# Row maxima of the first kv head moved into the projection, with two instead of three sets of query stacks

## The chip, the cores and the metric

The kernel runs on one core of a Trainium2 chip. The metric is the device time of one execution in microseconds (us); lower is better. TensorE (PE) multiplies matrices and writes to PSUM, VectorE (DVE), ScalarE (ACT) and GpSimd (POOL) work on tiles in SBUF, and SyncE (SP) issues most DMA transfers between DRAM and SBUF. Each engine works through its own instructions in their order and waits on semaphores for the others.

## What is computed

The reference is one transformer block on x of 2 x 1024 x 1024, fp32. Cut to what matters:

```python
xn = layernorm(x)                       # over the last axis
q = xn @ wq; k = xn @ wk; v = xn @ wv   # 32 query heads, 8 kv heads, 32 wide
q, k = rope(q), rope(k)                 # positions 0..1023
scores = q k^T / sqrt(32) + causal mask # four query heads share one kv head
s = (softmax(scores) @ v) @ wo
g = silu(ffn(xn))                       # gated, 4-bit weights with scales per group of 128
out = x + s * g
```

## The kernel before

The two sequences go through the same stages one after the other: `norm` (L301), `project` (L325), `attend` (L393) and `project_out` (L700). The feed-forward part follows for both together. The order of instructions in `norm`, `project` and `project_out` is set by a scheduler that puts ready work on each engine. In `attend` the order is the order of the code (`tc.manual_schedule()`).

**Projection.** The columns are done in ten blocks of 128: two for k, then v, then eight for q. `turned` does a k or q block in two halves of 512 tokens: eight fp32 products into one of three PSUM banks (`ps_qk`, L350), the rotation (two DVE instructions, L352 and L354, two on POOL, L355 and L356), a rounding to fp32r on ACT (`rot_hi`, L358), its remainder on DVE (`rot_lo`, L360), and two stores to DRAM (L361, L362), from SP. A score is computed from both parts. For the feed-forward part, xn is stored in two parts as well (`x_hi`, `x_lo`). In the first sequence, `look` prepares the scales of the 4-bit weights between the blocks (its tiles in `prep_ps`).

**Attention.** One of the eight kv heads is a round of its own, called a head here; its four query heads are j = 0 to 3. The scores need stacks: `kst_g`, the head's keys in 128 rows (both parts, each twice), and `qst_0` to `qst_3`, the four query heads' queries in 128 rows. They are loaded from DRAM by SP, four transfers of 128 KB for a tile (L414 and L422). The pool `at_q` holds three sets of the four query tiles (`bufs=3`, L402).

The softmax needs a shift for each row ahead of the exponential. `maxima` (L461 to L474) computes the scores with queries in rows: 48 units for a head, each one product (`s`) into one of two PSUM banks, on the diagonal a product that adds the mask (L470), and a row maximum on DVE (L474). `shifts` (L483 to L488) turns the maxima into three bf16 parts (`mt`), and `shift_rows` transposes them (`m_ps`, L502) and copies them to `mrow` (L506).

The head itself has 12 steps (qb, kt): two blocks of 512 queries, and the key tiles of 128 that each one sees (4 and 8). A step does the scores with keys in rows (`st`, L531, mask L540; one PSUM bank for each j), the product that adds the shifts (`weights`, L549), the exponential on ACT (L559), and, one step later, the product with v (`values`, L570). Sums for the denominator (`total`, L587) follow some steps later.

Into these steps the next head's maxima are woven. `turn` (L643) is called behind each score product and at the end of a step; it takes maxima units as long as a planned rate allows. So while head g computes, its DVE reductions and 48 units are for head g+1. The query stack of head g+1 is asked for at the start of head g. SP runs ahead of the other engines: such a load goes out as soon as its buffers are free. With three sets, the set of stack g+1 is that of stack g-2.

The maxima of head 0 have no head to be woven into. They run on their own, behind the projection:

```python
kst = [key_stack(0)]
stack = {0: stacks(0)}
for g in range(1, NKV):
    kst.append(key_stack(g))
mx = maxima_tile()
for _ in maxima(0, stack[0], mx):
    pass
box = [shift_rows(shifts(mx))]
```

Of the kernel before, what the change touches and what calls it, by code (L numbers as in the profile page):

```python
# [23 lines left out]
P = 128  # L24
# [12 lines left out]
def block_kernel(  # L37
# [141 lines left out]
    def scales_turned(pool, psp):  # L179
# [10 lines left out]
        ps = psp.tile([P, NF, 2, G_GU], F32, name="ps_sc")  # L190
# [14 lines left out]
        ps = psp.tile([P, NC, G_D], F32, name="ps_sd")  # L205
# [7 lines left out]
    def look(pool, psp):  # L213
# [19 lines left out]
        ps = psp.tile([1, 1], F32, name="ps_bad")  # L233
# [91 lines left out]
    def project(b, xnT, qs, ks, v, side):  # L325


        with tc.tile_pool(name="qkv_w", bufs=3) as wp, tc.tile_pool(name="qkv", bufs=3) as pool, tc.tile_pool(
# [16 lines left out]
            def turned(w, dst):  # L345
                for n in range(NB):
                    tok = slice(n * TB, (n + 1) * TB)
                    ps = psp.tile([P, TB], F32, name="ps_qk")
                    for s in range(NS):
                        nc.tensor.matmul(ps, w[:, s, :], xnT[:, s, tok], start=(s == 0), stop=(s == NS - 1))  # L350
                    t1 = pool.tile([P, TB], F32, name="rot1")
# [23 lines left out]
            for c in range(2):  # L375
                turned(following(), ks[c])
            for t in range(NT):
                ps = vps.tile([P, N_KV * HD], F32, name="ps_v")
                for s in range(NS):
                    nc.tensor.matmul(  # L380
                        ps, xnT[:, s, t * P : (t + 1) * P], w[:, s, :], start=(s == 0), stop=(s == NS - 1)
                    )
                nc.scalar.copy(v[:, t, :], ps)
            for c in range(NC):
                turned(following(), qs[c])
# [5 lines left out]
                nc.sync.dma_start(xs_dram[b][1, :, c, :], lo.bitcast(F32))  # L391

    def attend(qs, ks, v, oT):  # L393
# [5 lines left out]
        with ExitStack() as st:  # L399
            st.enter_context(tc.manual_schedule())  # L400
            kp = st.enter_context(tc.tile_pool(name="at_k", bufs=1))
            qp = st.enter_context(tc.tile_pool(name="at_q", bufs=3))  # L402
            pp = st.enter_context(tc.tile_pool(name="at_p", bufs=7))
            mp = st.enter_context(tc.tile_pool(name="at_m", bufs=1))
            sm = st.enter_context(tc.tile_pool(name="at_s", bufs=2))
            ps_s = st.enter_context(tc.tile_pool(name="ps_s", bufs=2, space=PSUM))
            ps_t = st.enter_context(tc.tile_pool(name="ps_t", bufs=1, space=PSUM))
            ps_o = st.enter_context(tc.tile_pool(name="ps_o", bufs=1, space=PSUM))

            def key_stack(g):  # L410
                k = kp.tile([P, T], F32R, name=f"kst_{g}")
                rows = slice(HD * (g % 4), HD * (g % 4 + 1))
                for i in range(4):
                    nc.sync.dma_start(k[HD * i : HD * (i + 1), :].bitcast(F32), ks[g // 4][i // 2, rows, :])  # L414
                return k

            def stacks(g):
                out = []
                for j in range(NREP):
                    q = qp.tile([P, T], F32R, name=f"qst_{j}")  # L420
                    for i in range(4):
                        nc.sync.dma_start(  # L422
                            q[HD * i : HD * (i + 1), :].bitcast(F32), qs[g][i % 2, HD * j : HD * (j + 1), :]
                        )
                    out.append(q)
                return out

            class Clock:  # L430
                pe = act = dve = 0.0
                bank = [0.0, 0.0]
                st = [0.0] * NREP

                def product(self, w, n=1.0, switch=False):
                    self.pe += 15.0 + 0.416 * n * w + (90.0 if switch else 0.0)

                def take(self):
                    self.pe = max(self.pe, self.bank[0])

                def read(self, ns):
                    self.dve = max(self.dve, self.pe + 180.0) + ns
                    self.bank = [self.bank[1], self.dve + 60.0]

                def exp(self, j, w):
                    self.act = max(self.act, self.pe + 180.0) + 170.0 + 0.84 * w
                    self.st[j] = self.act + 60.0

            clock = Clock()

            def maxima(g, q, mx):

                for qt in range(NT):
                    nk = (qt + 1) * P
                    for h, k0 in enumerate(range(0, nk, TB)):
                        k1 = min(nk, k0 + TB)
                        for j in range(NREP):
                            s = ps_s.tile([P, TB], F32, name="s")
                            diag = k1 == nk
                            clock.take()  # L460
                            nc.tensor.matmul(  # L461
                                s[:, : k1 - k0],
                                q[j][:, qt * P : (qt + 1) * P],
                                kst[g][:, k0:k1],
                                start=True,
                                stop=not diag,
                            )
                            clock.product(k1 - k0)
                            if diag:
                                nc.tensor.matmul(  # L470
                                    s[:, k1 - k0 - P : k1 - k0], ident_r, mask_q, start=False, stop=True
                                )
                                clock.product(P)
                            nc.vector.tensor_reduce(mx[:, qt, j, h : h + 1], s[:, : k1 - k0], AX.X, ALU.max)  # L474
                            clock.read(158.0 + 1.04 * (k1 - k0))
                            yield k1 - k0 + P

            def shifts(mx):


                mt = next(mts)
                nm = [sm.tile([P, NT, NREP, 2], F32, name=f"nm_{t}") for t in range(2)]
                nc.vector.tensor_reduce(nm[0][:, :, :, 0], mx, AX.X, ALU.max, negate=True)  # L483
                for t in range(3):
                    nc.vector.tensor_reduce(mt[:, :, :, t], nm[t % 2][:, :, :, :1], AX.X, ALU.max)
                    if t < 2:
                        nc.vector.tensor_reduce(nm[t][:, :, :, 1], mt[:, :, :, t : t + 1], AX.X, ALU.max, negate=True)
                        nc.vector.tensor_reduce(nm[1 - t][:, :, :, 0], nm[t], AX.X, ALU.add)  # L488
                clock.dve += 1700.0
                return mt  # L490

            mts = [mp.tile([P, NT, NREP, HD], BF16, name=f"mt_{i}") for i in range(2)]
            for mt in mts:
                nc.gpsimd.memset(mt, 0.0)
            mts = itertools.cycle(mts)

            def shift_rows(mt):
                mrow = mp.tile([P, T], BF16, name="mrow", bufs=2)
                for h in range(NB):
# [136 lines left out]
            for _ in maxima(0, stack[0], mx):  # L636
                pass
# [667 lines left out]
```

## Time and profile before

| what | us |
|---|---|
| runs of the kernel | 2524.58, 2527.64, 2533.06 |
| median of the runs | 2527.64 |
| the profiled execution, its own time | 2529.01 |
| its span in the trace | 2527.1 |

The mean granted clock of TensorE in the profiled execution is 0.959 of full speed. Times in the trace count from the start of the span. The page gives busy times of the engines, 40 slices of the span (in tenths, with the granted clock as PEclk), the chain of work that ended last, and groups of instructions. The trace behind it answers for a window, a tile or an engine's waits. The stages of the first sequence, by the trace: the last product of the projection ends at 201.84, the first score product of head 0 starts at 257.31, the first one of head 1 at 308.76, and project_out's products run from 642 to 752. In the second sequence, the projection's last product ends at 960.25 and the first score product starts at 1018.71.

### The profile page before, as it was taken

The page shows a single profiled execution, that of the slowest core. Times are in us where ns is not written, and L with a number is a line of the kernel's source. Part 1 is how long each engine was busy: PE and PEld are TensorE (multiplying, and loading weights), DVE is VectorE, ACT ScalarE, POOL GpSimd, SP SyncE. Part 2 cuts the span into 40 slices and gives each one's busy share as a digit, 9 for nine tenths or more (in the row PEclk, how much of TensorE's full clock was granted, in tenths as well). Part 3 has the DMA queues.
Part 4 walks back from the last instruction along what each step waited for, and adds up shares of the span by engine and source line. Part 5 has one row for each costly group of instructions (what it writes and reads, how often), then busy time and mean ns, then how long its engine had stood idle before and what let it go on. Part 6 is the DMA issues. An engine that isn't in the chain of part 4 may idle for free.

```text
span 2527.1 us, 32374 instructions
## 1 busy us (share of the span) xinstructions
PE 2402.1 (95%) x12130; PEld 1673.6 (66%) x12130; DVE 1407.3 (56%) x2176; ACT 1144.3 (45%) x1824; POOL 708.6 (28%) x449
## 2 busy tenths in 40 slices
PE   7997999999996996999999999999999999999997
PEld 4643565665784643565565787888887888888865
DVE  6144566663224234566663026676787777767865
ACT  2010344445343100344445135555578755556875
POOL 1231355546331231354546110000024400000352
PEclk8996899999997996899999999999999999999999
DMA  7357111200997327111110863222174655423465
GB/s 225 113 200 188 34 37 34 52 17 1 275 301 233 127 102 175 34 51 34 40 29 1 283 216 92 75 75 72 54 283 156 216 152 142 117 67 98 131 201 164
DMA packets 262350, 309.61 MB, mean 123 GB/s; under 512 B 18283, under 2 KB 202987, under 8 KB 262040
## 3 DMA queue, kind: packets, MB, share of 16 engines
q1 hardware_dynamic: 250964, 269.00, 36.0%
q0 software_dynamic: 9472, 33.83, 4.2%
q10 hardware_dynamic: 1748, 4.62, 0.6%
q8 instruction: 98, 1.61, 0.3%
q14 instruction: 68, 0.56, 0.1%
HBM read 214.58 MB, written 97.03 MB: 123 GB/s over the span
## 4 chain that ended last, share of the span: by engine, by line
PE 83%; DMA 6%; POOL 3%; issue 3%; DVE 2%; ACT 2%; SPq 1%; ACTq 0%; POOLq 0%; DVEq 0%
PE acc L984 25%; PE ps_qk L350 11%; PE acc L867 11%; PE s L461 9%; PE st L531 6%; PE o L570 5%; PE ps_wo L714 3%; DMA ng<-nf 3%; PE l L587 2%; PE ps_v L380 2%; PE st L549 2%; PE s L470 2%; PE st L540 1%; DVE mx L474 1%; DMA xt<-in_L_attn_x 1%
## 5 line engine op out<-in xcount | busy, mean ns | idle before, releaser
L984 PE MATMUL acc<-x,w 128*128 128x512 f32 x2752 | 640.0, 393 | 1.5 <-ACT gate L955 0.9
L984 PEld LDWEIGHTS acc<-x,w 128*128 128x128 f32 x2752 | 512.4, 188 | 120.7 <-DVE h L957 7.2
L474 DVE TENSOR_REDUCE mx<-s 128x1 f32<-128x512 f32 (+3 forms) x768 | 408.7, 556 | 257.9 <-PE s L470 196.8
L559 ACT ACTIVATE p<-st 128x512 f32<-128x512 f32 (+3 forms) x768 | 314.8, 497 | 510.6 <-PE st L549 507.2
L756 DVE TENSOR_SCALAR acc<-acc,r_gu 128x1024 f32<-128x1024 f32 x301 | 389.1, 1293 | 160.2 <-PE acc L984 158.1
L672 POOL TENSOR_TENSOR p<-p 128x1536 f32<-128x1536 f32 (+3 forms) x126 | 371.5, 2948 | 374.2 <-PE s L470 128.6
L754 ACT ACTIVATE acc<-acc,r_gu 128x1024 f32<-128x1024 f32 x301 | 327.5, 1088 | 230.3 <-PE acc L984 225.5
L461 PE MATMUL s<-kst,qst 128*128 128x512 f32 (+3 forms) x768 | 326.0, 444 | 43.5 <-DMA qst<-qs 37.7
L968 POOL TENSOR_TENSOR h_lo<-h,h_hi 128x512 fp32r<-128x512 f32 x78 | 100.3, 1287 | 820.9 <-PE acc L867 588.9
L461 PEld LDWEIGHTS s<-kst,qst 128*128 128x128 f32 x768 | 153.0, 202 | 216.4 <-issue 82.6
L350 PE MATMUL ps_qk<-xnT,w_qk 128*128 128x512 f32 x640 | 278.7, 596 | 0.7 <-ACT xnT L323 0.7
L756 DVE TENSOR_SCALAR acc<-acc,r_d 128x512 f32<-128x512 f32 x320 | 241.7, 759 | 67.1 <-PE acc L867 64.7
L531 PE MATMUL st<-qst,kst 128*128 128x512 f32 (+3 forms) x768 | 270.1, 385 | 2.8 <-ACT p L559 2.7
L754 ACT ACTIVATE acc<-acc,r_d 128x512 f32<-128x512 f32 x320 | 210.8, 662 | 65.6 <-PE acc L867 58.7
L867 PE MATMUL acc<-h_lo,w 128*128 128x512 f32 (+1 forms) x576 | 228.9, 397 | 2.9 <-POOL h_lo L968 2.6
L867 PE MATMUL acc<-h_hi,w 128*128 128x512 f32 (+1 forms) x576 | 229.5, 398 | 0.7 <-ACT h_hi L967 0.7
L714 PE MATMUL ps_wo<-oT,w_o 128*128 128x256 f32 x1024 | 226.6, 385 | 3.1 <-DVE oT L622 1.7
L350 PEld LDWEIGHTS ps_qk<-xnT,w_qk 128*128 128x128 f32 x640 | 122.2, 191 | 151.6 <-issue 149.7
L714 PEld LDWEIGHTS ps_wo<-oT,w_o 128*128 128x128 f32 x1024 | 197.7, 193 | 32.0 <-DVE oT L622 2.5
L531 PEld LDWEIGHTS st<-qst,kst 128*128 128x128 f32 x768 | 145.7, 192 | 41.7 <-ACT p L559 31.5
L570 PE MATMUL o<-p,v 128*32 128x512 f32 (+3 forms) x1536 | 164.6, 499 | 0.0
L358 ACT CAST rot_hi<-rot 128x512 fp32r<-128x512 f32 x40 | 24.7, 618 | 236.7 <-POOL rot L356 228.9
(154 smaller groups left out, 2198.1 us busy)
## 6 DMA issues: line engine op xcount, KB each, us to landing
w<-ng SPq DMA_DIRECT2D x86, 512.0 KB, 5.0
qst<-qs SPq DMA_DIRECT2D x256, 128.0 KB, 3.7
w<-nd SPq DMA_DIRECT2D x63, 512.0 KB, 3.6
ng<-nf POOLq DMA_DIRECT2D x42, 512.0 KB, 5.5
x<-xs SPq DMA_DIRECT2D x32, 512.0 KB, 6.8
xt<-in_L_attn_x SPq DMA_DIRECT2D x16, 512.0 KB, 5.1
w_qk<-in_L_attn_wq SPq DMA_DIRECT2D x16, 512.0 KB, 6.6
xs<-x_hi SPq DMA_DIRECT2D x16, 512.0 KB, 6.5
```

The lines of the kernel that those rows point to most:

```text
L350: nc.tensor.matmul(ps, w[:, s, :], xnT[:, s, tok], start=(s == 0), stop=(s == NS - 1))
L461: nc.tensor.matmul(s[:, : k1 - k0], q[j][:, qt * P : (qt + 1) * P], kst[g][:, k0:k1], start=True, stop=not diag,)
L474: nc.vector.tensor_reduce(mx[:, qt, j, h : h + 1], s[:, : k1 - k0], AX.X, ALU.max)
L531: nc.tensor.matmul(s[:, q0:], kst[g][:, kt * P : (kt + 1) * P], stack[g][j][:, qlo + q0 : qlo + TB], start=True, stop=False,)
L559: nc.scalar.activation(p[:, j, q0:], st[j][:, q0:], AF.Exp, scale=1.0 / math.sqrt(HD))
L570: nc.tensor.matmul(o[HD * j : HD * (j + 1), q0:], v[:, kt, HD * g : HD * (g + 1)], p[:, j, q0:], start=(kt == 0), stop=last,)
L672: what(*args)
L714: nc.tensor.matmul(ps[:, c, :], ws[c][:, g, :], oT[:, g, t0 : t0 + BLK], start=(g == 0), stop=(g == NS - 1))
L754: nc.scalar.mul(a, a, r)
L756: nc.vector.tensor_scalar(a, a, r, None, ALU.mult)
L867: nc.tensor.matmul(acc[c], w[:k, c * P : (c + 1) * P], ht[:k, :], start=(f == 0 and t == 0), stop=(t == 1), skip_group_check=(f > 0),)
L984: nc.tensor.matmul(a[:, n, :], w[i][:, g * P : (g + 1) * P], xs[t][:, g, n * TB : (n + 1) * TB], start=(g == 0 and t == 0), stop=(t == 1), ...
```

## The change

- The code of the maxima, the shifts and the loads of stacks moves out of `attend` into a class `Maxima`. Its tiles (`mt`, `kst_0`, a set `qst_0` to `qst_3`, `mx`, `nm`, `mrow`) lie in a pool `at_first`, opened before `norm`, and so do its two PSUM banks (`ps_s`). The fills of `mt` on POOL come before the projection.
- `project` loads `kst_0` behind the k blocks and the query stack of head 0 behind the first q block. From the third q block on, `turned` takes one maxima unit of head 0 after every second of its eight products. That is 48 units in six blocks. Then the shifts and `shift_rows` follow.
- The three PSUM tiles of `look` share one bank.
- `attend` starts with head 0's tiles given. It loads stack 1 first, then the keys of heads 1 to 7. `at_q` has two sets instead of three; the set of head 0 isn't used again. The stack of head g+1 is asked for at the start of head g for g of 1 and more.
- `turn` takes no units in steps 0, 1 and 2 of head 0 (`first_turn = 3`, counted over all steps).
- The pools of `attend`, of `project_out` (`wo`, `wo_ps`) and of `unpack` get `reuse_waits="tile"`: a tile waits for the users of its own bytes in what lay there earlier, and not for those of the whole pool.

In the lines of the changed kernel, the product of a unit is L477, its mask L486, its row maximum L488, the transposes of shifts L512, the copies to `mrow` L516, the loads of stacks L439 (keys) and L444 (queries), the score products L568 and L577, the shift product L586, the exponential L596, the products with v L607.

```diff
-            def turned(w, dst):
+            def turned(w, dst, work=iter(())):
                 for n in range(NB):
...
                     for s in range(NS):
                         nc.tensor.matmul(ps, w[:, s, :], xnT[:, s, tok], start=(s == 0), stop=(s == NS - 1))
+                        if s % 2:
+                            next(work, None)
...
             for c in range(2):
                 turned(following(), ks[c])
+            head.keys()
...
+            work = head.rows()
             for c in range(NC):
-                turned(following(), qs[c])
+                turned(following(), qs[c], work if c > 1 else iter(()))
+                if c == 0:
+                    head.queries()
...
+            for _ in work:
+                pass
...
+        def keys(self):
+            self.key_stack(0, self.k)
+
+        def queries(self):
+            self.query_stack(0, self.q)
+
+        def rows(self):
+
+            mx = self.tile()
+            yield from self.turns(self.k, self.q, mx)
+            mt = self.shifts(mx)
+            yield
+            self.rows_0 = self.shift_rows(mt)
...
-            kp = st.enter_context(tc.tile_pool(name="at_k", bufs=1))
-            qp = st.enter_context(tc.tile_pool(name="at_q", bufs=3))
-            pp = st.enter_context(tc.tile_pool(name="at_p", bufs=7))
...
+            kp = st.enter_context(tc.tile_pool(name="at_k", bufs=1, reuse_waits="tile"))
+            qp = st.enter_context(tc.tile_pool(name="at_q", bufs=2, reuse_waits="tile"))
+            pp = st.enter_context(tc.tile_pool(name="at_p", bufs=7, reuse_waits="tile"))
...
-            kst = [key_stack(0)]
-            stack = {0: stacks(0)}
-            for g in range(1, NKV):
-                kst.append(key_stack(g))
-            mx = maxima_tile()
-            for _ in maxima(0, stack[0], mx):
-                pass
-            box = [shift_rows(shifts(mx))]
+            stack = {0: head.q, 1: stacks(1)}
+            kst = [head.k] + [key_stack(g) for g in range(1, NKV)]
+            box = [head.rows_0]
...
-                while done < upto and most and clock.bank[0] <= clock.pe + 250.0:
+                while i >= first_turn and done < upto and most and clock.bank[0] <= clock.pe + 250.0:
...
+            first_turn = 3
             for i, (g, qb, kt) in enumerate(steps):
                 if qb == 0 and kt == 0:
                     if g + 1 < NKV:
-                        stack[g + 1] = stacks(g + 1)
-                        mx = maxima_tile()
-                        work = maxima(g + 1, stack[g + 1], mx)
+                        if g:
+                            stack[g + 1] = stacks(g + 1)
+                        mx = head.tile()
+                        work = head.turns(kst[g + 1], stack[g + 1], mx)
...
-        with tc.tile_pool(name="wo", bufs=NC) as wp, tc.tile_pool(name="wo_ps", bufs=2, space=PSUM) as psp:
+        with tc.tile_pool(name="wo", bufs=NC, reuse_waits="tile") as wp, tc.tile_pool(name="wo_ps", bufs=2, space=PSUM, reuse_waits="tile") as psp:
```

## The prediction, made before the changed kernel ran

> **What bounds the kernel now.** I read the page's busy times and slices first: TensorE is busy for 95% of the span, so the question is where the other 5% lies, and where TensorE is slow rather than idle.
>
> ```profile
> PE 2402.1 (95%) x12130; PEld 1673.6 (66%) x12130; DVE 1407.3 (56%) x2176; ACT 1144.3 (45%) x1824; POOL 708.6 (28%) x449
> ...
> PE   7997999999996996999999999999999999999997
> ...
> PEclk8996899999997996899999999999999999999999
> ```
>
> A slice is 63 us. The fourth (190 to 253 us) and the sixteenth (948 to 1011 us) lose both in busy time and in granted clock: these are the two entries into attention, one for each sequence. The list of TensorE's waits names what ends last there:
>
> ```profile
> PE s L461 <- DMA qst<-qs: 37.7, 8, 15.9
> ```
>
> 37.7 us in 8 waits, the longest 15.9: the maxima products wait for the query stacks to come back from DRAM. The chain of what ended last, in order of time, tells the first entry step by step (start, length, what):
>
> ```profile
> 194.95 6.88 PE ps_qk L350 x16
> 201.88 1.38 POOL mt L494 x2
> ...
> 207.68 2.04 DMA qs<-rot_lo
> ...
> 216.71 4.29 DMA qst<-qs
> ...
> 252.90 1.35 DVE mx L474 x2
> 256.51 1.03 PE m_ps L502 x8
> ```
>
> From the projection's last product (201.8) to the first transposes of the shifts (256.5) nothing runs that a head would count as progress, except the maxima. The windows by stage give clock and busy time (length; busy time of PE, weight load, DVE, ACT, POOL; granted clock; DMA share; GB/s):
>
> ```profile
> 202.00:257.00 55.00, 33.31 (x85) 20.94 (x86) 30.06 (x60) 1.90 (x2) 4.28 (x6) 0.55 0.85 201
> 257.00:268.00 11.00, 10.33 (x47) 7.09 (x45) 2.02 (x6) 3.70 (x8) 0.10 (x1) 0.50 0.00 0
> 268.00:600.00 332.00, 330.63 (x2468) 198.81 (x2467) 208.40 (x428) 146.54 (x354) 171.18 (x75) 1.00 0.13 33
> 643.00:648.00 5.00, 5.00 (x15) 4.02 (x14) 0.00 (x0) 0.00 (x0) 0.00 (x0) 0.56 1.20 290
> ```
>
> The entry runs at clock 0.55, and the next 11 us still at 0.50. After that the heads are bound by TensorE alone: busy 330.6 of 332 us at clock 1.00. Any wait put on TensorE there is a loss in full.
>
> **Part 1, the entry: what it gives.** I measure from the last ps_qk product (call it T) to the first score product of step 3 of head 0, since steps 0 to 2 are where the order changes. Before, that is 201.84 to 271.98, 70.1 us, for the first sequence and 960.25 to 1033.31, 73.1 us, for the second.
>
> After, the maxima, the key stack and the query stack are there already. What is left behind T: the rotation of the last block. Before, it ended at T+5.8 (rot_lo, 206.96 + 0.69), with the 1.38 us of the two fills of mt ahead of it on POOL, which now run before the projection; the shifts' rows (two copies, 0.76 us) stand behind it on DVE: T+6 to 7. The exponential's buffer lies on bytes that the last rot_lo store reads, which lands 2.04 us after its issue: T+8.3; ACT's table load (1.28 us at 206.95) comes next: first exponential at T+9.6. Before, 11.3 us lay between it (260.68) and step 3, with 11 maxima products of head 1 among them at half clock; without them, some 8, so T+18. There the first maxima product of head 1 needs stack 1 and kst_1: 20 transfers of 128 KB, issued from T+6.3; before, a stack's 16 issues took 8.3 us and each landed 3.3 us later, 20 thus 10.4 + 3.3 = 13.7: T+20. Then the 11 deferred products (0.25 us each, 2.75) and, since the clock comes back at T+26 at the earliest (6 us of dense work after T+20), 3 us lost to half clock: 25.75. Gain 44.4 us and 47.3 us.
>
> **What it costs in the projection.** The 48 maxima products and their masks now stand between ps_qk products, which were dense (81.8 of 82.0 us busy, clock 1.00), so they add in full. Start to start in the heads they take 0.23 us at 128 columns, 0.24 at 256, 0.29 at 384, 0.35 at 512 with a mask, 0.245 without: 13.0 us for 48. DVE must then read them: 48 reductions, 26.6 us by 0.29, 0.42, 0.55 and 0.69 each, in blocks where it was busy for 36 of 82 us. It has room, but there are two banks for s, and a rot_lo that waits on DVE for POOL and ACT holds the reductions behind it. In the first sequence some products stand in clumps around the preparation of scales. I take 4 us for that in the first sequence and 2 in the second (bounds: nothing, and 13.6, all that DVE's 26.6 exceed 13.0). Sums 17 and 15. Net gain 27.4 + 32.3 = 59.7; bounds 45 to 75.
>
> The fills of mt, the pools opened early and the shared prep_ps bank I cost at nothing: POOL is busy for 31 and ACT for 12 of 82 us of the projection. The looser waits of w_o and unpack I cost at nothing too: project_out's own products are dense from 642 to 752 us while its transfers fill 0.9 to 1.2 of the DMA engines, and the first w_o loads still wait for the last readers of attention.
>
> **Part 2, two buffers for the stacks: what it takes.** at_q goes from 3 to 2 sets. Set 0 of the first head now lies elsewhere, so stack 1 and 2 take the two, and stack 3 must wait until stack 1 is read for the last time: by the last step of head 1. Its maxima products stand in TensorE's queue right behind the first score product of head 2. So, too, stacks 4 to 7: five boundaries in each sequence, ten in all. Before, the same load was released one head (48 us) earlier than needed. The trace of before shows such a load (which nobody waited for then) beside the products that will wait for it:
>
> ```profile
> 306.56 0.33 PE L531 MATMUL st<-qst,kst 128*128 128x128 f32 x1
> 306.92 4.94 SPq L422 DMA_DIRECT2D qst<-qs  x11
> 309.25 0.33 PE L461 MATMUL s<-kst,qst 128*128 128x128 f32 x1
> 311.00 0.27 PE L461 MATMUL s<-kst,qst 128*128 128x128 f32 x1
> 311.31 0.39 PE L549 MATMUL st<-mrow,ones_b 32*128 32x512 bf16 x4
> ```
>
> The last reads of the old stack (306.56 to 307.28) release the issues; all 16 go out in 8.34 us (306.92 to 315.26), and each lands 3.1 to 3.6 us after its issue. The fourth tile is there at 318.2 or so; the product that reads it stood at 311.0. Queued behind it on TensorE are the weights of step 0 and everything else of the head: 7.2 us per boundary. The products of the three earlier tiles run singly meanwhile, one or two per 2 us.
>
> Then the clock. Where TensorE was busy for 4.3 of 9 us (634 to 643) the mean granted clock was 0.67, and the dense products after it ran at 0.56 for five more (window above); full clock came back after 4.4 to 6.8 us of dense work in six such places. Half of 5.6 us is 2.8. Per boundary 10.0, ten times 100 us. Bounds: the wait from 4.1 (16 issues at 0.303 us, as key stacks' have them, are out after 4.85 us and the last lands 3.3 later, at 315.1) to 8.8 (if transfers land after 4.5 us, as key stacks' did), the clock from nothing to 3.4: 4.1 to 12.2, or 41 to 122 in all. I take 10.0, as the row for the wait is the very load.
>
> The Trainium skill, page "TensorE: Matmul & The Clock Gate", section "Part 1: The HAM clock gate (the "warmup" mystery)", says that about 3.4 us of sustained work bring the full clock back. The trace's 4.4 to 6.8 are longer; by the page's figure each boundary would lose an estimated 1.7 us to the clock and not 2.8, and the time would be 11 us less. The page "Trainium Kernel Development and Optimization", section "Best Practices", asks for double buffers, by which two sets would do; the row above speaks against it, because a set comes free only in the instant in which the next one's first reader starts, and by the page the ten boundaries would cost nothing.
>
> **Sum.** 2529.0 (the profiled execution) - 59.7 + 100 = 2569.3. The median of the runs shown is 1.4 below the profiled execution; so 2568.
>
> **Rivals.**
> - The stalls come, but the single products keep the clock up: 7.2 x 10 = 72, net +12, 2540. For it: tiles land some 2 us apart, so TensorE is never idle for long at a stretch. Against: the half-busy stretch from 634 to 643 us.
> - DVE becomes the bound in the projection: all 13.6 us show in each sequence, 27 in place of 6: 2589. With bigger boundaries beside it, up to 2603. For it: rot_lo in front of reductions; against: DVE is busy for under half of that stage.
> - The other side: the stall is short, because the loads are released and land in time. The place is SP's queue at the five boundaries; it decides under 6.0 us per boundary (59.7 / 10). At the low bound of 4.1 the time is 2509, with no stall 2468. For it: key stacks' issues are that quick. Against: the release is the last read, and the row's load of 8.34 us ran with the DMA engines nearly idle (share 0.13), so little is left to speed it up.
> - The change doesn't do what it says: the maxima wait in the projection for their own stack, and TensorE stalls there instead (no gain, 100 lost): 2628. Against: two blocks, 27 us, lie between the store of head 0's queries and the first maxima product, and a stack needs 2 + 8.3 + 3.3.
>
> **Chances.** Forecast 0.60, clock up 0.13, DVE bound 0.13, short or no stall 0.10, no gain 0.04. About 0.3% (7.6 us) is what a measurement can tell from no change. Faster by more: 0.08 (most of the short-stall case); within: 0.06 (the rest of it and the lower end of the clock case); slower: 0.86. The range 2530 to 2603 leaves out the short stall, the no-gain case and a few ends of the others.
>
> **What would show it.** Right: TensorE's waits in the profile after have a line s <- DMA qst at L477 with some 10 to 40 waits and 60 to 85 us; PEclk falls below 9 in slices inside the heads; the first exponential of head 0 starts 9 to 11 us after the last ps_qk; the projection from block 2 on is 15 to 19 us longer; POOL and DVE don't become releasers there. Wrong: no such line inside the heads (then it is faster by about 60), or a wait of ps_qk or s for DVE of over 10 us in the projection. What would make it wrong most likely is the size of the stall at a boundary, since every microsecond there counts ten times.

## The result, and the profile after

| what | us |
|---|---|
| runs of the changed kernel | 2566.63, 2567.66, 2568.96, 2571.19 |
| their median | 2568.31 |
| median of the kernel before, run beside it | 2530.35 |
| ratio | 1.0154, 95% interval 1.0131 to 1.0177 |
| profiled execution after: its time, its span, mean granted clock | 2566.63, 2564.8, 0.954 |

The changed kernel is 38 us slower than before. The forecast was 2568, with a range of 2530 to 2603.

The page of the changed kernel, busy tenths and granted clock in 40 slices (a slice is 64 us now):

```profile
PE 2409.3 (94%) x12130; PEld 1690.3 (66%) x12130; DVE 1401.4 (55%) x2176; ACT 1144.5 (45%) x1824; POOL 708.5 (28%) x449
...
PE   7998998899996998999989999999999999999997
...
PEclk8998999889997998989999999999999999999999
```

The two dips at the entries have become shallower: slice 4 has 8 tenths instead of 7, slice 16 has 8 instead of 6, and their clocks are 8 instead of 6. In their place the heads show busy tenths of 8 in slices 7, 8 and 21 and clocks of 8 in slices 8, 9 and 18, where before there were only nines. TensorE's waits name what stands there:

```profile
PE s L477 <- DMA qst<-qs: 51.5, 40, 2.0
...
PE s L477 <- DMA kst<-ks: 9.4, 2, 6.1
```

Before, the first line read 37.7 us in 8 waits, the longest 15.9. Now it is 40 short ones. That is ten boundaries with four query tiles each, and no wait for a stack of head 0 is left. The timeline at one of them, the boundary of heads 2 and 3 of the first sequence (start, length, engine, line; in brackets the idle time before the instruction and what ended it):

```profile
385.65 7.26 SPq L444 DMA_DIRECT2D qst<-qs  x16
...
387.07 0.62 PE L512 MATMUL m_ps<-ident_b,mt 128*128 128x128 bf16 x8
387.50 0.48 PE L568 MATMUL st<-qst,kst 128*128 128x512 f32 x1
...
389.87 0.30 PE L477 MATMUL s<-kst,qst 128*128 128x128 f32 x1 [1.83 <-DMA qst<-qs]
...
392.07 0.30 PE L477 MATMUL s<-kst,qst 128*128 128x128 f32 x1 [1.45 <-DMA qst<-qs]
...
394.33 0.44 PE L477 MATMUL s<-kst,qst 128*128 128x128 f32 x1 [1.46 <-DMA qst<-qs]
...
396.44 0.44 PE L477 MATMUL s<-kst,qst 128*128 128x128 f32 x1 [0.82 <-DMA qst<-qs]
...
397.04 0.61 PE L586 MATMUL st<-mrow,ones_b 32*128 32x512 bf16 x4
```

The load of stack 4 goes out at 385.65, when head 2 reads stack 2 for the last time. Each of the four tiles is awaited singly. The fourth product stands at 396.44, that is 9.4 us behind the transposes of the boundary (m_ps, 387.07). Before, it stood 2.7 us behind them: the prediction shows it at 311.00, and the transposes were here:

```profile
308.33 0.62 PE L502 MATMUL m_ps<-ident_b,mt 128*128 128x128 bf16 x8
```

So 6.7 us are lost up to the fourth product. Over the ten boundaries its place is 9.5 us behind the transposes in the mean, and 2.7 before: 6.8 us. The windows of the same stretch (granted clock third from the end, then DMA share and GB/s) show what comes on top:

```profile
386.00:390.00 4.00, 2.17 (x27) 1.39 (x27) 0.76 (x2) 0.79 (x4) 3.53 (x3) 1.00 0.86 220
390.00:394.00 4.00, 1.42 (x8) 0.88 (x8) 0.58 (x2) 0.00 (x0) 0.00 (x0) 0.83 0.99 234
394.00:398.00 4.00, 2.85 (x18) 1.74 (x18) 0.58 (x2) 0.32 (x1) 0.00 (x0) 0.50 0.32 71
398.00:402.00 4.00, 4.00 (x23) 3.84 (x17) 1.70 (x4) 2.22 (x5) 0.00 (x0) 0.50 0.01 4
402.00:406.00 4.00, 4.00 (x29) 2.77 (x28) 2.14 (x4) 1.64 (x4) 0.73 (x1) 0.89 0.00 0
```

TensorE is busy for 1.42 of 4 us from 390 to 394, the clock is at 0.50 from 394 to 402, and dense work runs at half speed. The whole head takes 57.6 us and not 48.2. Over the ten boundaries a head loses 9.4 us: 6.8 up to the fourth product and 2.6 behind it.

From the first transposes of one boundary to those of the next, the two traces can be set side by side. Row by row, after less before, from the times of the last ps_qk product and of the boundaries:

| stretch | first sequence | second sequence |
|---|---|---|
| up to the last ps_qk product (second: from the end of head 6 of the first) | +13.1 | +13.3 |
| from there to the boundary of heads 0 and 1 | -41.7 | -42.9 |
| head 1 | +1.7 | +0.1 |
| heads 2 to 6, with the ten boundaries | +47.6 | +46.7 |

The sum is +37.8, with -0.1 behind it. The spans differ by 37.7. From its first ps_qk product to its last, the projection is 13.1 us longer in the first sequence and 12.1 in the second; the other 1.2 us of the second stand ahead of it.

At the first entry, in the timeline of the changed kernel:

```profile
219.09 1.01 PE L512 MATMUL m_ps<-ident_b,mt 128*128 128x128 bf16 x8 [1.68 <-DVE mt L500]
...
224.44 2.06 ACT L596 ACTIVATE p<-st 128x512 f32<-128x512 f32 x4
...
231.36 0.33 PE L568 MATMUL st<-qst,kst 128*128 128x128 f32 x1
...
235.15 0.33 PE L477 MATMUL s<-kst,qst 128*128 128x128 f32 x1 [3.35 <-DMA kst<-ks]
```

The last ps_qk product ends at 214.89. The first exponential starts 9.55 us later, step 3 of head 0 16.5 us later, and the first maxima product of head 1 20.3 us later, behind a wait of 3.35 us for kst_1, the tile that is loaded last.

At the other end of head 0 something else is new. Its 48 units (they are head 1's) now have nine steps instead of twelve. TensorE waits for DVE there, 2.1 us in three waits in each sequence, where before it was busy throughout. In the first sequence the clock is low behind them (windows as above):

```profile
274.00:280.00 6.00, 4.18 (x34) 2.74 (x35) 5.24 (x14) 0.79 (x4) 2.36 (x3) 1.00 0.00 0
280.00:283.40 3.40, 3.40 (x20) 2.89 (x17) 0.81 (x2) 0.00 (x0) 0.01 (x1) 0.50 0.02 5
```

Half of 3.4 us is the +1.7 of head 1 in the table. In the second sequence, behind the same waits, the clock stays at 1.00, and head 1 is as long as before.

### The profile page after: what moved, and what is told of

The parts are those of the page before. It is cut to its first block, busy times and chain, and to the rows that moved or that the text cites. A ratio compares the mean times of both kernels' runs of the same rounds, so it can differ in the third digit from the quotient of the medians.

```text
span 2564.8 us, 32366 instructions
## 1 busy us (share of the span) xinstructions
PE 2409.3 (94%) x12130; PEld 1690.3 (66%) x12130; DVE 1401.4 (55%) x2176; ACT 1144.5 (45%) x1824; POOL 708.5 (28%) x449
## 4 chain that ended last, share of the span: by engine, by line
PE 68%; issue 12%; DMA 7%; POOL 6%; SPq 3%; DVE 3%; ACT 2%; POOLq 0%; ACTq 0%; DVEq 0%
PE acc L1014 25%; PE acc L897 10%; PE s L477 8%; PE st L568 6%; PE o L607 5%; PE ps_wo L744 3%; DMA ng<-nf 3%; PE l L624 2%; PE st L586 2%; SPq L444 2%; POOL rot L357 2%; DMA qst<-qs 2%; POOL rot L358 2%; PE s L486 1%; PE st L577 1%
## 5 line engine op out<-in xcount | busy, mean ns | idle before, releaser
L488 DVE TENSOR_REDUCE mx<-s 128x1 f32<-128x512 f32 (+3 forms) x768 | 407.6, 555 | 342.4 <-PE s L486 286.2
L596 ACT ACTIVATE p<-st 128x512 f32<-128x512 f32 (+3 forms) x768 | 314.8, 497 | 518.6 <-PE st L586 515.2
L477 PE MATMUL s<-kst,qst 128*128 128x512 f32 (+3 forms) x768 | 345.7, 466 | 67.4 <-DMA qst<-qs 51.5
L477 PEld LDWEIGHTS s<-kst,qst 128*128 128x128 f32 x768 | 154.7, 204 | 244.0 <-issue 119.7
L350 PE MATMUL ps_qk<-xnT,w_qk 128*128 128x512 f32 x640 | 292.4, 597 | 0.7 <-ACT xnT L323 0.7
L568 PE MATMUL st<-qst,kst 128*128 128x512 f32 (+3 forms) x768 | 286.0, 406 | 7.1 <-ACT p L596 5.2
L784 ACT ACTIVATE acc<-acc,r_d 128x512 f32<-128x512 f32 x320 | 210.8, 662 | 66.2 <-PE acc L897 59.2
L568 PEld LDWEIGHTS st<-qst,kst 128*128 128x128 f32 x768 | 155.3, 204 | 48.8 <-ACT p L596 36.3
L607 PE MATMUL o<-p,v 128*32 128x512 f32 (+3 forms) x1536 | 167.6, 508 | 0.0
```

The costliest lines, as they stand in the source:

```text
L477: nc.tensor.matmul(s[:, : k1 - k0], q[j][:, qt * P : (qt + 1) * P], k[:, k0:k1], start=True, stop=not diag,)
L568: nc.tensor.matmul(s[:, q0:], kst[g][:, kt * P : (kt + 1) * P], stack[g][j][:, qlo + q0 : qlo + TB], start=True, stop=False,)
L596: nc.scalar.activation(p[:, j, q0:], st[j][:, q0:], AF.Exp, scale=1.0 / math.sqrt(HD))
L607: nc.tensor.matmul(o[HD * j : HD * (j + 1), q0:], v[:, kt, HD * g : HD * (g + 1)], p[:, j, q0:], start=(kt == 0), stop=last,)
L784: nc.scalar.mul(a, a, r)
```

## The experiments

The theory: the entry's gain and the ten stalls are independent of each other, and two sets make the stalls, because the load of stack g+1 is released by the last reader of stack g-1 and awaited at once. The rivals: something else in the change lengthens the heads (the pools, the order of the loads, SP's queue), or the heads lose to the clock alone. Each ratio is against the kernel before, run beside. Its median was 2531.0 beside the two sets alone, the third set, the later reader with two sets, and the two queues. It was 2529.8 beside the later reader with three sets, the added products, the key tile first with first_turn 0, and the best version; and 2528.3 beside the other four.

**Only the two sets, in the kernel before.**

```diff
-            qp = st.enter_context(tc.tile_pool(name="at_q", bufs=3))
+            qp = st.enter_context(tc.tile_pool(name="at_q", bufs=2))
```

> The kernel before with two sets of query stacks instead of three, and nothing else. Theory (two sets make the stall): all eight stacks share the two sets here, so stacks 2 to 7 are each released by the last score product of the head before the one in which they are read: six boundaries in each sequence, twelve in all. At 9.4 us each, as the head intervals of the changed kernel show (57.6 against 48.2), 113 us more than before: about 2643, with some 48 waits of s for qst in the heads. Rival (the new pools, the order of loads or the later start of the maxima lengthen the heads, and two sets would do): within 8 us of 2530.

Measured: 2645.26, ratio 1.0465 (1.0437 to 1.0492). Its TensorE waits:

```profile
PE s L461 <- DMA qst<-qs: 99.3, 56, 15.6
```

These are 48 waits more than the 8 of before, as twelve boundaries make them. Its heads take 57.5 to 58.9 us from the first boundary on. One number in the kernel before makes the stall, with none of the other parts there.

**A third set out of what lies idle.**

```diff
-                out = [qp.tile([P, T], F32R, name=f"qst_{j}") for j in range(NREP)]
+                out = head.q if g % 3 == 0 else [qp.tile([P, T], F32R, name=f"qst_{j}") for j in range(NREP)]
```

> The changed kernel with the first head's four query tiles used again as a third set, for the stacks of heads 3 and 6; no byte more is taken. Theory: the ten stalls go, heads take 48.2 us again, and what is left is the gain at the two entries: 2568 - 94 = 2474. Rival (the load goes out late for another reason, such as its place in SP's queue): the waits stay and the time is 2568.

Measured: 2475.61, ratio 0.9785 (0.9769 to 0.9801). The list of TensorE's waits, from its top:

```profile
PE ps_ln L322 <- DVE rstd L316: 17.7, 2, 15.7
PE ps_ln L322 <- DVE mv L312: 11.2, 5, 3.3
PE ps_ln L322 <- DVE xn L318: 10.0, 2, 7.1
PE s L477 <- DMA kst<-ks: 9.5, 2, 6.2
```

The line of s and qst is gone and heads 2 to 6 take 48.2 us. The loss in them is 0.0 us instead of 94.3. What is left is the gain alone, 55 us on the kernel before, and it is the better kernel of the two by far.

**Two sets, but the reader later in every head.**

```diff
-                while i >= first_turn and done < upto and most and clock.bank[0] <= clock.pe + 250.0:
+                while i % 12 >= first_turn and done < upto and most and clock.bank[0] <= clock.pe + 250.0:
```

> The changed kernel with two sets, but in every head, not only the first, no maxima are taken in steps 0, 1 and 2. Theory: the load is released as late as before, but its reader stands some 10 us later, when nearly all tiles have landed (11 us after the last read of the old stack), so most of the 94 us come back: 2474 to 2490, the rest being up to 1.5 us of DVE or landing waits in each head. Rival (the stall is not the place of the reader; or 48 units don't fit into nine steps and DVE becomes the bound): over 2530.

Measured: 2534.72, ratio 1.002 (1.0007 to 1.0033). That is what the rival gave (over 2530), in the second of its forms. No wait for qst is left, so the reader's place does remove the stall. But heads 1 to 6 take 52.5 to 55.8 us, since 48 units don't fit into nine steps. The timeline at the end of head 2 and its windows:

```profile
380.65 0.50 PE L477 MATMUL s<-kst,qst 128*128 128x512 f32 x1 [0.55 <-DVE mx L488]
...
381.99 0.50 PE L477 MATMUL s<-kst,qst 128*128 128x512 f32 x1 [0.19 <-DVE mx L488]
...
386.24 1.03 PE L512 MATMUL m_ps<-ident_b,mt 128*128 128x128 bf16 x8 [1.46 <-DVE mt L500]
```

```profile
374.00:378.00 4.00, 4.00 (x32) 2.55 (x28) 3.20 (x6) 1.12 (x4) 2.98 (x1) 1.00 0.01 4
378.00:382.00 4.00, 3.23 (x23) 1.16 (x15) 2.35 (x5) 1.04 (x4) 2.90 (x3) 1.00 0.00 0
382.00:386.00 4.00, 2.74 (x24) 1.81 (x24) 3.60 (x11) 0.79 (x4) 0.78 (x1) 1.00 0.39 109
386.00:390.00 4.00, 3.76 (x21) 3.01 (x21) 1.03 (x3) 0.00 (x0) 0.49 (x1) 0.57 0.97 223
```

The last six units stand in a row on two banks, and TensorE waits for DVE to have read a bank (the two lines at L477). The shifts come later for it, and the transposes wait 1.46 us for them. TensorE is idle for 2.0 of 8 us from 378 to 386, and then the clock is at 0.57 for 4 us. The two are told apart by whole heads: one at whose start the clock stays up, one at whose start it falls, and a head of the kernel before:

```profile
547.15:599.68 52.53, 49.82 (x360) 29.16 (x361) 29.80 (x62) 21.58 (x52) 24.53 (x11) 1.00 0.14 31
386.24:440.29 54.05, 51.34 (x360) 30.46 (x361) 29.88 (x62) 21.69 (x52) 24.56 (x12) 0.97 0.17 41
308.33:356.56 48.23, 48.02 (x364) 28.96 (x361) 30.07 (x62) 21.58 (x54) 23.92 (x12) 1.00 0.17 44
```

The head of 52.5 us loses 4.3 us at full clock. TensorE is idle for 2.7 us in it and not 0.2, and the same products keep it busy for 49.8 us and not 48.0; why they take 1.8 us more is open. A fall of the clock adds 1.5 us. To see whether a piece of the load hides in it, the same with three sets:

> Three sets, and in every head no maxima in steps 0, 1 and 2. With two sets this form (a_late) left 2535 instead of the 2474 to 2490 expected, with heads of 52.5 to 54 us and no wait for a transfer. If squeezing 48 units into nine steps is what costs (units in a row on two banks ahead of the shifts, then a clock that falls at the head's end), it costs the same with three sets: heads of 52.5 to 54 us, 2528 to 2542. If a rest of the load is in it, three sets bring heads near 48.2 us: under 2490.

Measured: 2539.13, ratio 1.0037 (1.0022 to 1.0051), heads of 52.5 to 55.8 us. The load has no part in it. 48 units in nine steps cost what 48 units in twelve do not.

**Which resource sets the length of the load.**

```diff
-                    nc.sync.dma_start(
+                    (nc.scalar if g > 2 and i % 2 else nc.sync).dma_start(
```

> The changed kernel with every second of the 16 transfers of stacks 3 to 7 issued from ACT's queue instead of SP's. It asks what sets the length of the load. If it is SP's issues (0.46 us each, 7.3 for 16, as the prediction worked it out), they are out in half the time and the wait falls by some 3.5 us at each of ten boundaries: 2533. If it is the DMA engines themselves (share 0.99 at 234 GB/s between 390 and 394 us in the changed kernel), the tiles land as late as before: 2568, within 6 us.

Measured: 2571.3, ratio 1.0164 (1.0147 to 1.0181): no gain. One boundary (TensorE's timeline) and its window:

```profile
393.35 0.30 PE L477 MATMUL s<-kst,qst 128*128 128x128 f32 x1 [3.51 <-DMA qst<-qs]
...
397.25 0.45 PE L477 MATMUL s<-kst,qst 128*128 128x128 f32 x1 [0.97 <-DMA qst<-qs]
```

```profile
388.00:392.00 4.00, 1.84 (x24) 1.03 (x23) 0.76 (x2) 0.79 (x4) 3.34 (x3) 1.00 0.80 242
392.00:396.00 4.00, 1.77 (x8) 1.45 (x8) 0.58 (x2) 0.00 (x0) 0.00 (x0) 0.78 1.05 239
```

The list has 24 waits of 45.0 us in all and not 40 of 51.5. But the fourth product stands as late as with one queue (9.5 us behind the transposes), the engines move 239 GB/s at a share of 1.05, and the head is as long as before (57.2 to 58.3 us). The condition of the first theory didn't come about, though:

```profile
387.45 4.93 SPq L444 DMA_DIRECT2D qst<-qs  x8
388.65 0.36 ACTq L444 DMA_DIRECT2D qst<-qs  x1
389.05 5.58 ACTq L444 DMA_DIRECT2D qst<-qs  x7
```

SP now needs 0.62 us for an issue instead of 0.45, ACT starts 1.2 us later, and the 16 issues take 7.2 us as they did from one queue (7.26). So a second queue doesn't help. That the DMA engines hold both queues back fits their share of about 1, but the run can't tell it from another limit that the queues have in common. The Trainium skill, page "Trainium Kernel Development and Optimization", section "Key Constraints", says that transfers issued from several queues run on the same 16 engines, so that only issue time is saved. This run agrees that the transfers are no faster, with 2571.3 against 2568.3; issue time wasn't saved either.

**Wait and clock, separated.**

```diff
+        def turns(self, k, q, mx, warm=None):
...
+                        if warm and qt == 0:
+                            for _ in range(6):
+                                nc.tensor.matmul(s, warm[1][j][:, :P], warm[0][:, :TB], start=True, stop=True)
...
+                        work = head.turns(kst[g + 1], stack[g + 1], mx, (kst[g], stack[g]) if g > 1 else None)
```

> The changed kernel (two sets, ten stalls) with 24 more products at each of the ten boundaries: six of 512 columns ahead of each of the first four maxima products of heads 3 to 7, on the stacks of the head that runs, into the bank that the maxima product then overwrites. They change no result; they fill TensorE's waits (some 1.5 us each) while the stack lands. It separates the two terms of a boundary's 9.4 us. Theory: the wait of 6.7 us stays, since the tiles land when they do, and the 2.7 us that follow at half clock go: heads 2 to 6 take 54.5 to 55.5 us, 2538 to 2545 in all. Rival (the 2.7 us are not the clock's, but maxima that are late): 2568, or more by what the added products cost (5.9 us at each boundary if nothing hid them: 2627).

Measured: 2548.49, ratio 1.0074 (1.0057 to 1.009). Transposes and fourth product at the boundary of the timeline above (1 us earlier here), and its windows:

```profile
386.16 0.62 PE L515 MATMUL m_ps<-ident_b,mt 128*128 128x128 bf16 x8
...
396.15 0.33 PE L480 MATMUL s<-kst,qst 128*128 128x128 f32 x1 [0.22 <-DMA qst<-qs]
```

```profile
386.00:390.00 4.00, 3.81 (x28) 2.76 (x23) 1.05 (x3) 0.53 (x4) 2.66 (x3) 1.00 0.95 238
390.00:394.00 4.00, 3.58 (x18) 2.43 (x16) 0.29 (x1) 0.00 (x0) 0.00 (x0) 1.00 1.03 229
394.00:398.00 4.00, 3.78 (x30) 2.60 (x29) 0.89 (x3) 1.05 (x3) 0.00 (x0) 1.00 0.16 37
398.00:402.00 4.00, 4.00 (x31) 2.69 (x30) 2.41 (x6) 2.85 (x8) 0.00 (x0) 1.00 0.00 0
```

TensorE is busy for nearly all of it, and the clock stays at 1.00, in the 20 us behind each of the ten boundaries. Heads 2 to 6 lose 73.0 us in all, by the same reckoning that gave 94.3: 7.3 us each and not 9.4. All 7.3 are lost up to the fourth product, which stands 9.9 us behind the transposes in the mean (10.0 here) and not 9.5. So the 2.6 us that the changed kernel loses behind that product are the clock's: at full clock they are gone. The added products delay the fourth product by 0.4 us; that is all that shows of the 5.9 us that they need. More work made the kernel 20 us faster.

**What the entry's gain is made of.** From here on all versions have the third set (2475.61 without further edits).

Without maxima in the projection (they follow it, with the stacks there):

```diff
-                turned(following(), qs[c], work if c > 1 else iter(()))
+                turned(following(), qs[c], iter(()))
```

> The three-set version (a_ring, 2475.6) without maxima in the projection: the first head's stacks are loaded early as there, but its 48 units follow behind the last block. It splits the gain at the entries into early loading and hiding. Per sequence the projection gets 13 us shorter, and 48 units stand in the open: DVE's 26.6 us of reductions, some 28 to 30 as in the kernel before; the wait for kst_1 (3.4 and 6.1 us) goes. Theory: 9 to 13 us slower in each sequence, 2494 to 2502, so that most of the entry's gain is the early load. Rival (the hiding is all): the full 27 us and more in each, over 2525.

Measured: 2497.84, ratio 0.9878 (0.9862 to 0.9895). That is 22 us more, as the theory had it. Of the 55 us that three sets gain on the kernel before, 22 are the hiding of the maxima in the projection. Some 33 come from the stacks that are there in time, and from what else the change has.

Without the delay of the first head's turns:

```diff
-            first_turn = 3
+            first_turn = 0
```

> The three-set version with first_turn 0: in head 0 the first maxima product of head 1 stands behind the first score product of step 0, and waits there for the stack and the key tile that are loaded behind the projection. Theory: TensorE stands until these land (about 20 us behind the projection's end), with the steps 0 to 2 behind them instead of ahead: 7 to 10 us more in each sequence, 2490 to 2496. Rival (the three steps cost the same either way, since the clock is low in both): within 4 us of 2475.6.

Measured: 2473.86, ratio 0.9782 (0.9766 to 0.9798). It cannot be told from 2475.61, so my theory fell here. The wait for kst_1 grew as expected, from 9.5 to 21.5 us, 6 us in each sequence. Against it stands what the delay itself costs. With twelve steps for the units, TensorE's 2.1 us of waits for DVE at the end of head 0 are gone in both sequences, and so are the 1.7 us of half clock in head 1 of the first. The rest I put down to the entry, where TensorE has little to do in the meantime (at the first one it waits 3.2 us for the exponentials of step 0 in either version) and the clock is low; this is argued.

With the key tile of head 1 loaded ahead of its query stack:

```diff
-            stack = {0: head.q, 1: stacks(1)}
-            kst = [head.k] + [key_stack(g) for g in range(1, NKV)]
+            kst = [head.k, key_stack(1)]
+            stack = {0: head.q, 1: stacks(1)}
+            kst += [key_stack(g) for g in range(2, NKV)]
```

> The three-set version with the key tile of head 1 loaded ahead of its query stack instead of behind it. The first unit then needs the first five transfers and not all 20; the fourth unit still needs the last. Theory: the waits for kst_1 (3.3 and 6.2 us) shrink to some 1 and 3 us of waits for qst, since they are taken one by one: 2471 to 2474. Rival (the load as a whole sets it): 2475.6, within 1.5.

Measured: 2464.65, ratio 0.9744 (0.9727 to 0.976). That is 11 us and not 2 to 4. The waits shrink from 9.5 to 3.6 us. In the first sequence TensorE, then at work from 228 us on, has the full clock from 234, where the version with only the third set has it from 246 (its first transposes stand at 222.1, here at 220.7). Head 0 takes 54.7 instead of 60.6 us. I had priced the wait and left out the clock. By the traces, head 0 is 5.9 us shorter in the first sequence and 3.2 in the second; the other 2 us aren't accounted for.

The same with first_turn 0:

> Three sets, the key tile of head 1 loaded ahead of its query stack (2464.7 with first_turn 3), and first_turn 0. With the key tile last, first_turn 0 or 3 made no difference that could be measured (2473.9 and 2475.6), although the wait for kst_1 grew from 9.5 to 21.5 us. If the three steps matter only when there is other work for TensorE while tiles land, it is here that they count, because here nothing waits in step 3: 6 to 12 us slower than 2464.7, 2470 to 2477. Rival: first_turn never matters, 2463 to 2467.

Measured: 2468.78, ratio 0.9757 (0.974 to 0.9773). It is 4 us above 2464.65, with intervals that overlap. By the profile, head 0 takes 60.2 and 62.0 us instead of 54.7 and 59.2, and head 1 gets 1.7 and 0.1 back, its half clock again. So the delay is worth a few us where nothing waits in step 3. That it matters in the time is likely, but not shown.

Without "tile" reuse in the pools (all `reuse_waits="tile"` taken out):

> The three-set version without reuse_waits in any of the pools: a tile waits for all users of the pool that lay there. It prices the last part of the change. Theory: the loads of stack 1 and the score banks wait for the last store of the projection (2 us after its issue) as the first exponential of the first sequence does anyway: 1 to 4 us in each sequence, 2478 to 2484. Rival (the part matters, since the stacks and w_o wait for whole stages): over 2490.

Measured: 2487.5, ratio 0.9832 (0.9816 to 0.9849), 12 us more, between what the theory and the rival gave. This edit took out more than the change had put in: two PSUM pools of the feed-forward part have had the option before too. The stretch behind the last boundary of the second sequence is 8.8 us longer in this version (1177.1 against 1168.3), and that part can't be put down to the change. Up to there it is 3.5 us, against the 2 to 8 expected.

The best version (third set, first_turn 3, key tile of head 1 in a tile of its own, loaded beside that of head 0):

```diff
+            self.k1 = pool.tile([P, T], F32R, name="kst_1")
...
+            self.key_stack(1, self.k1)
...
-            kst = [head.k] + [key_stack(g) for g in range(1, NKV)]
+            kst = [head.k, head.k1] + [key_stack(g) for g in range(2, NKV)]
```

> Three sets, first_turn 3, and the key tile of head 1 loaded inside the projection beside that of head 0, in a tile of its own of 4 KB per partition, which the attention then has less. The entry then waits for 16 transfers instead of 20, the query tiles first. Theory: the entry's waits are almost gone when the key tile comes first (3.6 us in all, in the second sequence), so it gains 0 to 4 us on 2464.7: 2460 to 2465. Rival (20 transfers crowd the engines, and the clock comes back later for it): under 2458.

Measured: 2454.09, ratio 0.9706 (0.9692 to 0.9721), 76 us faster than the kernel before. That is below the theory's range and in the rival's, but the entry gives only 5 us of it: head 0 of the second sequence takes 54.1 us (59.2 with the key tile first in the attention). Another 8.6 us, against the version with only the third set, come between the sequences: from the last boundary of the first to the last ps_qk product of the second it takes 366.9 us, against 375.5. First load of x and first product of the second norm, there and here:

```profile
732.26 2.21 SPq L307 DMA_DIRECT2D xt<-in_L_attn_x  x2
747.66 3.37 PE L322 MATMUL ps_ln<-ident,xn 128*128 128x128 f32 x16 [15.65 <-DVE rstd L316]
```

```profile
598.83 0.35 SPq L307 DMA_DIRECT2D xt<-in_L_attn_x  x1
728.65 3.67 PE L322 MATMUL ps_ln<-ident,xn 128*128 128x128 f32 x16 [6.75 <-ACT oT L752]
```

There, all eight loads of x go out when project_out is nearly through, and TensorE waits 15.65 us for the statistics. Here six of the eight go out between 598 and 661, and the wait is 6.75 us. These 8.9 us account for the 8.6. Why the loads go out earlier is argued only: a tile more in the early pool changes where other tiles lie, and so what the loads of x wait for. No run separates it from the entry.

## Why the prediction was right

| step of the prediction | predicted | measured |
|---|---|---|
| first exponential behind the last ps_qk product | 9.6 | 9.55 |
| kst_1 landed, behind the same | 20 | 20.3 |
| projection longer, first and second sequence | 17 and 15 | 13.1 and 13.3 (1.2 of the latter ahead of the projection) |
| entry shorter, head 1 included | 44.4 and 47.3 | 40.0 and 42.8 |
| net gain | 59.7 | 56.4 |
| wait at a boundary, up to the fourth product | 7.2 | 6.8 |
| clock at a boundary, behind it | 2.8 | 2.6 |
| ten boundaries | 100 | 94.3 |
| sum by the profiled executions | +40.3 | +37.7 |

- **The bound and the mechanism** stood: in heads that TensorE bounds, each wait is lost in full. One edit that made room, two sets in place of three, cost more than the edit that it made room for had gained. Two experiments show it from both ends: two sets alone, and the third set back.
- **The number** is closer than its terms. The entry's gain was 8.9 us too high, the projection's cost 5.6 too high and the ten boundaries 5.7 too high, and these errors nearly cancel. That the median is 0.3 us from 2568 is luck; that the stalls outweigh the gain is not. The bounds of 45 to 75 for the net gain don't follow from the terms beside them, which give 38.5 to 65.7.
- **The projection**: the products' 13.0 us were about right (the prediction's rows add up to 12.8; 13.1 and 12.1 came). The 4 and 2 us for DVE's queue did not come: TensorE waits for a row maximum 2.4 us in the first 220 us, and not at all that the list shows between 900 and 1010. In four other profiles with this projection the first one is 1.4 to 2.4 us longer, so some of the 4 us can come. The sign of 15 to 19 us was missed. The rival in which DVE becomes the bound is out.
- **The entry**: the gain was too high by 4.4 and 4.5 us. One term was put at nothing: head 1's units in nine steps of head 0. It shows as 2.1 us of waits for DVE at the end of head 0 in each sequence, and 1.7 us of half clock behind them in the first. The rest is a wait and the clock. I put the clock's return at 26 us behind the last product. In the first sequence it is still at 0.80 from 240 to 246 (25 to 31 us behind), after the wait for kst_1. The wait for kst_1 is 3.35 us there and 6.1 in the second sequence, where I had TensorE arrive 2 us ahead of it. That these terms make up the whole difference in their sizes was not worked out.
- **The wait at a boundary** was worked out from the load in the trace of before, and the size nearly holds. The sign for it didn't: the list shows 51.5 us and not 60 to 85, since it counts only the idle 5.15 us of a boundary, and not the products that run between the waits. The reason beside it was wrong. I wrote that this load ran with the DMA engines nearly idle (share 0.13) and that SP's issues set its length. 0.13 is the mean over all heads. During the load, the trace of before has a share of 0.93 at 226 GB/s (311 to 315.3), and in the run with two queues the 16 issues take as long as from one. So a queue doesn't issue at a pace of its own here, and the lower bound of 4.1 us, from quicker issues, was no bound.
- **The clock**: 2.6 us, between the bounds of 0 and 3.4. The rival in which it stays up lost: it stayed up when TensorE was given work, by the added products. By the Trainium skill, page "TensorE: Matmul & The Clock Gate", section "Part 1: The HAM clock gate (the "warmup" mystery)", it would have been an estimated 1.7; the measured value is nearer to mine.
- **The advice of double buffers** that the prediction weighed: two sets cost 114 us in the kernel before (2645.26 against 2531.04), so the row of the trace decided rightly.

## What to carry to other kernels

Count buffers by the time between the last read of the old content and the first read of the new one: if both stand side by side at a boundary, most of the load's length is exposed there (here 6.8 us, with 10.8 us from the first issue to the fourth product), and it counts once for each boundary. When a change needs room, look for a tile that has become idle before you take a buffer from a pool that feeds the bound engine. A gap on TensorE is to be priced with its aftermath: here 2.6 us of half clock beside 6.8 us of waiting, and 11 us in all for one tile that was loaded last and not first.

## What the runs showed of the hardware beyond that

- The clock falls without a long gap. At the boundary shown, no idle time of TensorE is over 1.83 us, yet the clock is at 0.83 and then 0.50 with TensorE busy for 1.42 and 2.85 of 4 us. The Trainium skill, page "TensorE: Matmul & The Clock Gate", section "Why this matters for your kernels", advises against idle gaps of over some 3 us. Here gaps of half that length did it, in a row. The later reader shows the same with busy shares of 3.23 and 2.74 in 4 us and no gap over 1.46: 0.57 behind them. Nor does the clock fall each time: behind the same 2.1 us of waits at the end of head 0 it goes to 0.50 for 3.4 us in the first sequence and stays at 1.00 in the second. So the longest gap alone doesn't tell it; what does was not measured.
- Filler products pay. 24 products of 512 columns at a boundary, in time that was idle, made the kernel 20 us faster by keeping the clock at 1.00.
- While 16 transfers of 128 KB land, the DMA engines are at a share of 0.99 to 1.05 and 234 to 239 GB/s, from one queue as from two. In the prediction's row of 643 to 648 us other transfers reach 290 GB/s at 1.20, so what holds this load at 234 is open.
